# One denominator product per block for all groups and heads, and a turn at the tile's end, in a two-layer graph attention kernel

## The chip, the cores and the metric

The kernel runs on one core of a Trainium2 chip. The metric is the device time of one execution in microseconds (us), as a median of several runs. A profile is one execution, recorded by the hardware profiler, with the start and length of each instruction and of each DMA packet.

## The reference

The input has 3327 nodes with 1024 features and an adjacency matrix that is symmetric, has a full diagonal and is sparse: about 16 edges per node. There are two layers, each of the form x = layernorm(x + attention(x)).

```python
# layer 0: 8 heads of 128
h = (x @ W).reshape(C, H, D)
e = leaky_relu(alpha_src[:, :, None] + alpha_dst[:, None, :], 0.2)   # alpha = h . a, per head
attn = softmax(where(adj == 0, -inf, e), axis=-1)
out = einsum('hij,hjd->hid', attn, h_heads)
x = layernorm(x + out)
# layer 1: one head of 1024
h = x @ W1
att = softmax(where(adj > 0, leaky_relu(f1 + f2.T), -9e15), axis=1)  # f = h . a1, h . a2
x = layernorm(x + relu(att @ h))
```

For each target node and each head, layer 0 needs two sums over the node's edges: the weighted sum of the sources' rows, and the sum of the weights alone, which is the softmax's denominator. The change is about the second.

## The kernel before

The nodes are padded to 26 tiles of 128 targets. A first phase (`proj`) multiplies x with the weights, writes the rows of layer 0 to `h0_d` (1024 features and 16 exponentials of scores), and turns the adjacency matrix into lists of edges: for each tile `NB` = 17 lists of 128 edges, in `idx` (source row), `tgt` (target) and `re_d` (the target's factor per head). A tile's 128 targets form `NG` = 4 groups of `GT` = 32. Each of the `EB` = 4 blocks holds one list of 128 edges for each group; the 17th list, the end block, takes what is left over for the whole tile. If the lists would not suffice, another arm of the program (`by_pairs`) would run; here it does not.

The phase `sparse` has two stages, both under `pipeline`, with the order of the instructions on each engine written out by hand (`tc.manual_schedule`): the instructions stand on an engine's queue in the order in which Python issues them. The first stage has `Layer0` for its tiles and runs from about 482 to 1185 us of the span; the second has `Target` (layer 1).

For a tile t and block b, `pipeline` issues: at b = 0 `own()` of this tile; then `weights(b + 1)` (after the last block `weights(0)` of the next tile); then `sums(b)`; then the gathers of block b of the next tile; then one step of `work`, the `finish` of the tile before; and, while there are any, one step of `ahead` (`score_weights`, L767, at the start of layer 0).

- `gather` (L803): four indirect DMAs of 128 rows each, one per group, from GpSimd's queue into one of five buffers `src`; the end block has one such DMA into one of two buffers `end`.
- `weights` (L858): VectorE makes the edge's weight per head, `wp` (L865, L866), ScalarE copies it to `w` (L868), and VectorE spreads it over a one-hot matrix of the targets, `e` (L870): 128 edges x (4 groups x 8 heads x 32 targets).
- `sums` (L876): for each head and group a product `e`^T x rows into the group's 32 partitions of `acc` (L898); for the end block a product over all 128 partitions per head (L882). At b = 1 and 2 the tile's own rows, scaled by ScalarE in `own` (L850), are added by a product with the identity (L890), which stands ahead of that block's sums on TensorE.
- The denominators (L904 to L910): for each block and group, the one-hot matrix of the group's edges (`oh`, 128 x 32) is the stationary side, and the weights (`w`, 128 x 8) are the moving side; the result goes to the group's 32 partitions of `den`, which is 128 targets x 8 heads. Block 0's products are issued with block 1's; the end block has one product over all targets (L886). `den` has a single PSUM buffer (tag "S", one bank).
- `finish` (L915): the denominators' inverse `ri` (L918, L919); per head, the sums are scaled by it and added to x in `y` (L924); a step ends; statistics and square root (L192 to L195); a step ends; normalisation (L199) and a first score product (L931); a step ends; a second score product (L931), two exponentials (L936, L937), and the store of the row to `y_d`, on SP's queue (L938). Layer 1's gathers read `y_d`.

`pipeline` runs one step of `finish` after each block (`behind` is one for each), so that tile t's four steps follow the blocks 0 to 3 of tile t + 1; the last tile's steps run after the loop.

Of the kernel before, what the change touches and what calls it, by code (L numbers as in the profile page):

```python
# [9 lines left out]
F32 = mybir.dt.float32  # L10
# [3 lines left out]
AF = mybir.ActivationFunctionType  # L14
OP = mybir.AluOpType
AX = mybir.AxisListType
# [3 lines left out]
P = 128  # L20
# [6 lines left out]
def kernel(  # L27
# [28 lines left out]
    nc = tc.nc  # L56
    N, D = x.shape
    H, DH = a0_src.shape
# [10 lines left out]
    GT = 32  # L69
    NG = P // GT  # L70
    EB = 4
# [30 lines left out]
    ident = const.tile([P, P], F32, name="ident")  # L102
# [54 lines left out]
    class Phase:  # L157
# [7 lines left out]
        def bank(self, tag, shape, name, dt=F32):  # L165
            return self.psum.tile(shape, dt, tag=tag, name=name, bufs=self.banks[tag])

        def sbuf(self, tag, shape, bufs, name=None, dt=F32):
            return self.pool.tile(shape, dt, tag=tag, name=name or tag, bufs=bufs)
# [283 lines left out]
    with ExitStack() as own, tc.manual_schedule():  # L453
        ph = Phase(own, "proj", {"A": 2, "S": 1, "T": 2})
        pool, bank = ph.pool, ph.bank
# [205 lines left out]
        for t in range(3, NT):  # L661
# [3 lines left out]
            if t == 12:  # L665
                n, own = NT - 1, pool.tile([P, NT], I32, bufs=1, name="own")
# [76 lines left out]
    def sparse(own):  # L743
        ph = Phase(own, "sparse", {"A": 5, "S": 1, "T": 1, "E": 1})
        pool, bank, sbuf = ph.pool, ph.bank, ph.sbuf
# [14 lines left out]
        nc.vector.memset(none_b, 0.0)  # L760
        io_t = ph.iota([P, P], [[1, P]], "io_t", base=1)


        wc = pool.tile([P, 2, KT], F32, bufs=1, name="wc")
        wa = [pool.tile([P, D], F32, bufs=1, name=f"wa{n}") for n in range(2)]
# [60 lines left out]
        class Layer0:  # L826
# [31 lines left out]
            def weights(self, b):  # L858

                s = self.src[b]  # L860
                ng, wide = (NG, GT) if b < EB else (1, P)
                blk = slice(b * NG, b * NG + ng)
                oh = self.oh[:, blk, :] if b < EB else self.oh2.unsqueeze(1)
                wp = way[:, (b % 4) * NG * H : (b % 4 * NG + ng) * H].rearrange("p (g h) -> p g h", g=ng)
                nc.vector.tensor_tensor(wp, s[:, :, D : D + H], self.re[:, blk, :], OP.mult)  # L865
                nc.vector.tensor_tensor(wp, wp, s[:, :, D + H : D + 2 * H], OP.max)  # L866
                w = sbuf("w", [P, NG, H], 4)[:, :ng]
                nc.scalar.activation(w, wp, AF.Copy)  # L868
                e = sbuf("e", [P, H * P], 3).rearrange("p (g h t) -> p g h t", g=ng, h=H)
                nc.vector.tensor_tensor(  # L870
                    e, oh.unsqueeze(2).to_broadcast([P, ng, H, wide]),
                    wp.unsqueeze(3).to_broadcast([P, ng, H, wide]), OP.mult,
                )
                self.made[b] = w, e

            def sums(self, b):  # L876
                w, e = self.made[b]
                rowsof = self.src.pop(b)[:, :, :D].rearrange("p g (h d) -> p g h d", h=H)
                first = b == 0
                if b == EB:  # L880
                    for h in range(H):
                        nc.tensor.matmul(  # L882
                            self.acc[h // 4][:, h % 4, :], e[:, 0, h, :], rowsof[:, 0, h, :],
                            start=False, stop=h % 4 == 3,
                        )
                    nc.tensor.matmul(self.den, self.oh2, w[:, 0, :], start=False, stop=True)  # L886
                    return

                if b in (1, 2):
                    nc.tensor.matmul(  # L890
                        self.acc[b - 1].rearrange("p h d -> p (h d)"), ident, self.h[:, (b - 1) * HALF : b * HALF],
                        start=False, stop=False,
                    )
                elif b == 3:
                    nc.tensor.matmul(self.acc[0][:, 0, :1], ident_b, none_b, start=False, stop=False)
                for h in range(H):
                    for g in range(NG):
                        nc.tensor.matmul(  # L898
                            self.acc[h // 4][g * GT : (g + 1) * GT, h % 4, :], e[:, g, h, :], rowsof[:, g, h, :],
                            start=first and h % 4 == 0, stop=False,  # L900
                        )

                if b == 1:
                    self.den = bank("S", [P, H], "den")  # L904
                for n in (0, 1) if b == 1 else (b,)[: b]:
                    for g in range(NG):
                        nc.tensor.matmul(
                            self.den[g * GT : (g + 1) * GT, :], self.oh[:, n * NG + g, :], self.made[n][0][:, g, :],
                            start=n == 0, stop=False,
                        )  # L910

            def close(self):
                pass

            def finish(self):  # L915

                ri = sbuf("ri", [P, H], 2)
                nc.vector.tensor_tensor(ri, self.den, self.es, OP.add)  # L918
                nc.vector.reciprocal(ri, ri)  # L919
                t, row = self.t, self.y  # L920
                y = row[:, :D]
                for h in range(H):
                    yh = y[:, h * DH : (h + 1) * DH]
                    nc.vector.scalar_tensor_tensor(  # L924
                        yh, self.acc[h // 4][:, h % 4, :], ri[:, h : h + 1], yh, op0=OP.mult, op1=OP.add
                    )
                yield
                yield from ph.norm_steps([y])
                for n in range(2):
                    pr = sbuf("pr", [P, D], 1)  # L930
                    nc.vector.scalar_tensor_tensor(  # L931
                        pr, y, 1.0, wa[n], op0=OP.mult, op1=OP.mult, accum_out=r1.sd[:, t, n, :]
                    )
                    if n == 0:
                        yield
                nc.scalar.activation(row[:, D + 1 : D + 2], r1.d[:, t, :], AF.Exp)  # L936
                nc.scalar.activation(row[:, D + 2 : D + 3], r1.d[:, t, :], AF.Exp, scale=SLOPE)  # L937
                nc.sync.dma_start(y_d[t * P : (t + 1) * P, :], row)  # L938
# [267 lines left out]
    with arm.Else():  # L1206
        with ExitStack() as own:
            sparse(own)
# [23 lines left out]
```

## Time and profile before

| | us |
|---|---|
| median of 3 runs | 1957.28 |
| lowest, highest | 1956.42, 1968.05 |
| the profiled execution | 1903.19 |
| its span | 1901.5 |

In the profiled execution TensorE is busy for 1518.5 us (80%), VectorE for 1146.6, GpSimd for 1030.2 and ScalarE for 546.6. The granted clock of TensorE is 0.905 on average, about 0.8 in layer 0's edge stage and 1.0 in layer 1. The DMA engines read 578.85 MB and write 42.97 MB.

The engines are named PE (TensorE), DVE (VectorE), ACT (ScalarE), POOL (GpSimd) and SP; PEld is PE's weight load. A group's line names the source line, the engine, the operation, destination<-sources, the shapes, the number, then busy us and mean ns. A line of waits tells who waited for whom, with the total in us, the number of times and the longest. A line of the chain has a start, a length, and what ran or was waited for. A line of the timeline has a start, a length, engine, source line, operation, destination<-sources and the number; in brackets the idle time before it and what ended that.

### The profile page before, as it was taken

How to read it: one execution, taken by the hardware profiler on the slowest of the kernel's cores; microseconds unless marked ns; L12 is line 12 of the kernel's file. 1: busy time of each engine (PE TensorE's matmuls, PEld its weight loads, DVE VectorE, ACT ScalarE, POOL GpSimd, SP SyncE). 2: the span in 40 equal slices, each digit the busy share in tenths (PEclk: the TensorE clock that was granted, in tenths of full speed). 3: DMA queues.
4: the chain of work that ended last, by engine and by line, in shares of the span. 5: the costliest groups of instructions: out<-in, count | busy, mean ns of one | idle time of the engine just before them, and what ended most of it. 6: DMA issues, size and time to landing. Idle time of an engine off the chain costs nothing.

```text
span 1901.5 us, 38079 instructions
## 1 busy us (share of the span) xinstructions
PE 1518.5 (80%) x14663; PEld 902.4 (47%) x14663; DVE 1146.6 (60%) x3058; ACT 546.6 (29%) x1422; POOL 1030.2 (54%) x1391
## 2 busy tenths in 40 slices
PE   8799999999266555656556565399999999999997
PEld 5465556666255554545545454144444444444443
DVE  6699999986386665666666666244444444444442
ACT  5544455542022222222222222012222212222220
POOL 4322222220576666676676764677766667666650
PEclk9899999999678777787788877699999999999999
DMA  7656455411899999999999997899999999999980
GB/s 184 101 133 131 100 99 99 88 62 39 325 373 404 396 392 394 366 405 392 386 392 389 394 376 273 332 398 410 400 372 382 380 378 369 359 371 373 366 326 33
DMA packets 171068, 567.76 MB, mean 299 GB/s; under 512 B 27690, under 2 KB 34346, under 8 KB 170878
## 3 DMA queue, kind: packets, MB, share of 16 engines
q0 software_dynamic: 131056, 455.68, 67.6%
q1 hardware_dynamic: 39822, 109.56, 15.4%
q8 instruction: 118, 1.93, 0.4%
q14 instruction: 72, 0.59, 0.1%
HBM read 578.85 MB, written 42.97 MB: 327 GB/s over the span
## 4 chain that ended last, share of the span: by engine, by line
PE 52%; DMA 24%; DVE 12%; ACT 6%; issue 4%; POOL 2%; SPq 0%; DVEq 0%; ACTq 0%; POOLq 0%
DMA src<-h_d,idx 20%; PE mm L1025 20%; PE acc L993 12%; PE mm L479 12%; DVE e L870 3%; PE acc L898 3%; ACT junk L311 3%; PE tr L176 2%; POOL src L803 2%; DMA src<-y_d,idx 2%; DVE pr L931 1%; PE acc L882 1%; DMA wt<-in_L_gnn_W_dram 1%; ACT xT L179 1%; PE xp L411 1%
## 5 line engine op out<-in xcount | busy, mean ns | idle before, releaser
L803 POOL DMA_INDIRECT src<-h_d,idx x416 | 441.1, 1060 | 209.1 <-PE acc L898 58.0
L803 POOL DMA_INDIRECT src<-y_d,idx x416 | 415.7, 999 | 221.6 <-PE acc L993 96.3
L898 PE MATMUL acc<-src,e 128*32 128x128 f32 x6656 | 278.5, 337 | 253.6 <-DVE e L870 253.5
L479 PE MATMUL mm<-wt,xT 128*128 128x347 f32 (+1 forms) x1248 | 402.3, 469 | 3.3 <-DMA wt<-in_L_gnn_W_dram 2.9
L1025 PE MATMUL mm<-wt,xT 128*128 128x512 f32 x832 | 383.3, 604 | 0.8 <-DVE o L1028 0.8
L898 PEld LDWEIGHTS acc<-src,e 128*32 128x32 f32 x6656 | 234.8, 137 | 311.3 <-DVE e L870 284.3
L479 PEld LDWEIGHTS mm<-wt,xT 128*128 128x128 f32 x1248 | 228.3, 192 | 106.0 <-issue 4.2
L1025 PEld LDWEIGHTS mm<-wt,xT 128*128 128x128 f32 x832 | 152.2, 190 | 199.5 <-issue 179.1
L993 PE MATMUL acc<-src,es 128*32 128x342 f32 (+1 forms) x2496 | 206.2, 464 | 33.8 <-DVE es L984 31.0
L870 DVE TENSOR_TENSOR e<-oh,way 128x1024 f32<-128x1024 f32 x130 | 158.7, 1221 | 63.2 <-ACT w L868 62.8
L993 PEld LDWEIGHTS acc<-src,es 128*32 128x32 f32 x2496 | 71.6, 111 | 158.6 <-issue 112.9
L868 ACT ACTIVATE w<-way 128x32 f32<-128x32 f32 (+1 forms) x130 | 24.6, 189 | 407.7 <-DVE way L866 395.6
L1028 DVE SCALAR_TENSOR_TENSOR o<-mm,y 128x512 f32<-128x512 f32 x52 | 35.9, 691 | 166.2 <-PE mm L1025 166.2
L1007 ACT ACTIVATE z<-y,ri 128x342 f32<-128x342 f32 (+1 forms) x78 | 39.5, 570 | 313.9 <-DVE ri L1003 313.9
L865 DVE TENSOR_TENSOR way<-src,re 128x32 f32<-128x32 f32 x104 | 20.8, 200 | 175.1 <-DMA src<-h_d,idx 157.6
L179 ACT ACTIVATE xT<-tr 128x512 f32<-128x512 f32 x104 | 59.4, 596 | 151.0 <-PE tr L176 150.9
L981 DVE TENSOR_TENSOR way<-way,src 128x128 f32<-128x128 f32 x104 | 31.1, 299 | 90.0 <-ACT way L951 44.2
L850 ACT ACTIVATE own<-own,es 128x128 f32<-128x128 f32 x208 | 63.6, 388 | 57.4 <-DVE es L847 57.4
L311 ACT ACTIVATE junk<-ad 128x3328 uint8<-128x3328 uint8 x26 | 78.4, 3014 | 2.5 <-POOL ad L308 2.5
L882 PE MATMUL acc<-end,e 128*128 128x128 f32 x416 | 67.7, 328 | 13.3 <-DVE e L870 13.3
L296 POOL CAST mvs<-r 128x8 bf16<-128x8 f32 x26 | 6.0, 232 | 122.8 <-ACT r L295 122.8
L335 POOL TENSOR_TENSOR place_of<-cnt 128x1 f32<-128x1 f32 x26 | 4.9, 190 | 121.0 <-ACT cnt L328 101.5
(188 smaller groups left out, 1959.7 us busy)
## 6 DMA issues: line engine op xcount, KB each, us to landing
h_d<-ht SPq DMA_DIRECT2D x26, 520.0 KB
own<-h_d SPq DMA_DIRECT2D x26, 520.0 KB
y_d<-y SPq DMA_DIRECT2D x26, 514.0 KB
y<-y_d SPq DMA_DIRECT2D x26, 514.0 KB
x<-in_x_dram SPq DMA_DIRECT2D x25, 512.0 KB
y<-in_x_dram SPq DMA_DIRECT2D x25, 512.0 KB
out_dram<-o SPq DMA_DIRECT2D x25, 512.0 KB
ad<-in_adj_dram POOLq DMA_DIRECT2D x25, 415.9 KB
```

The lines of the kernel that those rows point to most:

```text
L176: nc.tensor.transpose(tr[:, k, :], src[:, (4 * g + k) * P : (4 * g + k + 1) * P], ident)
L179: nc.scalar.activation(part, tr, AF.Copy)
L311: nc.scalar.activation(junk, ad, AF.Copy, accum_out=self.deg)
L479: nc.tensor.matmul(acc, xT[t][:, k, :], wt[:, k, CUTS0[c] : CUTS0[c + 1]], start=k == 0, stop=k == KT - 1)
L803: nc.gpsimd.indirect_dma_start(out=s[:, g, :w], out_offset=None, in_=table[:, :], in_offset=bass.IndirectOffsetOnAxis(ap=idx[:, t, b * NG ...
L850: nc.scalar.activation(hn, hn, AF.Copy, scale=es[:, n : n + 1])
L870: nc.vector.tensor_tensor(e, oh.unsqueeze(2).to_broadcast([P, ng, H, wide]), wp.unsqueeze(3).to_broadcast([P, ng, H, wide]), OP.mult,)
L882: nc.tensor.matmul(self.acc[h // 4][:, h % 4, :], e[:, 0, h, :], rowsof[:, 0, h, :], start=False, stop=h % 4 == 3,)
L898: nc.tensor.matmul(self.acc[h // 4][g * GT : (g + 1) * GT, h % 4, :], e[:, g, h, :], rowsof[:, g, h, :], start=first and h % 4 == 0, stop= ...
L993: nc.tensor.matmul(self.acc[c][to, :m], es[:, g, :], s[:, g, CUTS[c] : CUTS[c + 1]], start=b == 0, stop=b == EB,)
L1007: nc.scalar.activation(z[:, cut], self.res[:, cut], AF.Copy, scale=ri[:, 1:2])
L1025: nc.tensor.matmul(acc, xT[:, k, :], wt1[:, k, half], start=k == 0, stop=k == KT - 1)
```

## The change

A block's denominators are now one product for all groups and heads: `w` (128 edges x 32 columns, group by head) is the stationary side, and the whole one-hot matrix (128 edges x 128 targets) is the moving side. The result has group and head in the partitions (32) and the targets in the columns; of each row only the 32 columns of its own group mean anything. The end block's weights are copied four times (`to_broadcast`), so that its product has the same form. In `finish`, VectorE multiplies the 32 x 128 result with a mask, `meets`, that keeps each group's own targets, into `met`; and a further product turns `met` by a 32 x 8 matrix `heads` of ones into 128 targets x 8 heads, in columns of the same bank. A `yield` after that makes `finish` five steps in place of four. Mask and `heads` are made once from the identity.

```diff
@@ sparse
+        meets = pool.tile([NG * H, P], F32, name="meets")
+        nc.vector.tensor_reduce(meets..., ident[: NG * H, : NG * H]..., AX.X, OP.max)
+        nc.vector.tensor_copy(meets...[:, :, 1:], meets...[:, :, :1].to_broadcast(...))
+        heads = pool.tile([NG * H, H], F32, name="heads")
+        nc.vector.tensor_reduce(heads, ident[: NG * H, : NG * H].rearrange("p (g h) -> p h g", g=NG), AX.X, OP.max)
@@ weights
-                w = sbuf("w", [P, NG, H], 4)[:, :ng]
-                nc.scalar.activation(w, wp, AF.Copy)
+                w = sbuf("w", [P, NG, H], 4)
+                nc.scalar.activation(w, wp if b < EB else wp.to_broadcast([P, NG, H]), AF.Copy)
@@ sums
-                    nc.tensor.matmul(self.den, self.oh2, w[:, 0, :], start=False, stop=True)
+                    nc.tensor.matmul(
+                        self.den[: NG * H, :P], w.rearrange("p g h -> p (g h)"), self.oh2, start=False, stop=True
+                    )
...
-                    self.den = bank("S", [P, H], "den")
+                    self.den = bank("S", [P, P + H], "den")
                 for n in (0, 1) if b == 1 else (b,)[: b]:
-                    for g in range(NG):
-                        nc.tensor.matmul(
-                            self.den[g * GT : (g + 1) * GT, :], self.oh[:, n * NG + g, :], self.made[n][0][:, g, :],
-                            start=n == 0, stop=False,
-                        )
+                    nc.tensor.matmul(
+                        self.den[: NG * H, :P], self.made[n][0].rearrange("p g h -> p (g h)"),
+                        self.oh[:, n * NG : (n + 1) * NG, :].rearrange("p g t -> p (g t)"),
+                        start=n == 0, stop=False,
+                    )
@@ finish
+                met = sbuf("met", [NG * H, P], 2)
+                nc.vector.tensor_tensor(met, self.den[: NG * H, :P], meets, OP.mult)
+                nc.tensor.matmul(self.den[:, P:], met, heads, start=True, stop=True)
+                yield
                 ri = sbuf("ri", [P, H], 2)
-                nc.vector.tensor_tensor(ri, self.den, self.es, OP.add)
+                nc.vector.tensor_tensor(ri, self.den[:, P:], self.es, OP.add)
```

More of the change, by code (lines that the diff above doesn't have):

```diff
@@ L761, in sparse @@
         io_t = ph.iota([P, P], [[1, P]], "io_t", base=1)
+        meets = pool.tile([NG * H, P], F32, name="meets")
+        nc.vector.tensor_reduce(
+            meets.rearrange("p (g t) -> p g t", g=NG)[:, :, 0], ident[: NG * H, : NG * H].rearrange("p (g h) -> p g h", g=NG),
+            AX.X, OP.max,
+        )
+        nc.vector.tensor_copy(
+            meets.rearrange("p (g t) -> p g t", g=NG)[:, :, 1:],
+            meets.rearrange("p (g t) -> p g t", g=NG)[:, :, :1].to_broadcast([NG * H, NG, GT - 1]),
+        )
+        heads = pool.tile([NG * H, H], F32, name="heads")
+        nc.vector.tensor_reduce(
+            heads, ident[: NG * H, : NG * H].rearrange("p (g h) -> p h g", g=NG), AX.X, OP.max
+        )
         wc = pool.tile([P, 2, KT], F32, bufs=1, name="wc")
@@ L885, in sums @@
                         )
-                    nc.tensor.matmul(self.den, self.oh2, w[:, 0, :], start=False, stop=True)
+                    nc.tensor.matmul(
+                        self.den[: NG * H, :P], w.rearrange("p g h -> p (g h)"), self.oh2, start=False, stop=True
+                    )
                     return
@@ L903, in sums @@
                 if b == 1:
-                    self.den = bank("S", [P, H], "den")
+                    self.den = bank("S", [P, P + H], "den")
                 for n in (0, 1) if b == 1 else (b,)[: b]:
-                    for g in range(NG):
-                        nc.tensor.matmul(
-                            self.den[g * GT : (g + 1) * GT, :], self.oh[:, n * NG + g, :], self.made[n][0][:, g, :],
-                            start=n == 0, stop=False,
-                        )
+                    nc.tensor.matmul(
+                        self.den[: NG * H, :P], self.made[n][0].rearrange("p g h -> p (g h)"),
+                        self.oh[:, n * NG : (n + 1) * NG, :].rearrange("p g t -> p (g t)"),
+                        start=n == 0, stop=False,
+                    )
             def close(self):
```

## The prediction

> **What bounds the kernel now.** The edit touches layer 0's edge stage alone, which runs from the first gather at 482 us to about 1185 us. I first read the busy table in stretches (columns: stretch, length, busy us of PE, its weight loads, DVE, ACT, POOL, then PE clock, DMA share, GB/s).
>
> ```profile
> 555.00:560.00 5.00, 5.00 (x147) 4.62 (x147) 4.59 (x9) 1.46 (x2) 1.67 (x2) 0.85 0.59 215
> 850.00:950.00 100.00, 59.51 (x1171) 50.17 (x1172) 63.04 (x154) 23.12 (x65) 67.15 (x65) 0.76 1.01 391
> 1170.00:1185.00 15.00, 11.04 (x246) 9.62 (x246) 12.44 (x30) 4.16 (x9) 0.00 (x0) 0.86 0.25 97
> ```
>
> In the body of the stage the 16 DMA engines are full (share 1.01, 391 GB/s) while no compute engine passes 67%. Two places differ: a dip at 555 us, and the last 15 us, where the gathers are over. Then the waits of PE, and the chain of waits in the body.
>
> ```profile
> PE acc L898 <- DVE e L870: 237.6, 93, 6.3
> ...
> 888.49 8.95 DMA src<-h_d,idx
> 897.44 0.02 issue
> 897.47 0.02 POOLq L803
> 897.48 0.01 issue
> 897.49 9.66 DMA src<-h_d,idx
> ```
>
> PE spends 237.6 us waiting for the edge weights `e`. In the chain a gather lands and releases the next one: transfer follows transfer, about 10 us each, with compute only now and then between. The question is then whether a later PE would hold a gather back. A gather of block b writes the buffer read five blocks before. The timeline shows how long that buffer has been free (L803 is a gather, L898 the block sums, L907 the denominators, L890 the injection of the own row, L918 the start of `finish`):
>
> ```profile
> 902.52 0.16 DVE L918 TENSOR_TENSOR ri<-den,es 128x8 f32<-128x8 f32 x1
> 902.66 1.95 PE L898 MATMUL acc<-src,e 128*32 128x128 f32 x64 [1.35 <-DVE e L870]
> 903.98 0.99 POOL L803 DMA_INDIRECT end<-h_d,idx  x1 [0.30 <-issue]
> 904.43 0.29 PE L907 MATMUL den<-w,oh 128*32 128x8 f32 x16
> 918.37 1.70 POOL L803 DMA_INDIRECT src<-h_d,idx  x1 [0.30 <-PE acc L898]
> 926.05 1.13 PE L890 MATMUL acc<-own,ident 128*128 128x512 f32 x2
> ```
>
> `sums(1)` ends at 904.61. After the `end` gather at 903.98 come eight gathers, the next tile's blocks 0 and 1, and then, at 918.37, the first that needs block 1's buffer: 13.8 us later. Counted alike from the same timeline, blocks 0, 2 and 3 give 12.4, 11.7 and 12.1 us. So in the body PE may be some 10 us late before DMA loses anything. The name PE behind 0.30 us of idle time is misleading: 0.30 stands before gathers that wait for nothing, too. At 558 us it is not so: there POOL stood 4.15 us behind PE, while the step-wise `score_weights` filled DVE.
>
> [...]the denominators' 8 columns have a median of 176 ns, the sums' 128 columns 273. [...]LDWEIGHTS (loading the stationary operand):[...] here 113 ns for 32 columns, 192 for 128.[...] the full 5 us stretches here show 403 to 412[...].
>
> **The change, part by part.** A product shows as two instructions (104 blocks x 4 groups = 416 products, 832 rows).
>
> *Removed:* per tile 16 group products and one of the end block, 34 rows. The 16 rows at 904.43 took 0.30 us with their loads at full clock (19 ns each), eight at half clock 0.41 us. That is 0.6 to 1.6 us for the groups, 0.4 for the end: 1.0 to 2.0 us a tile.
>
> *Added products:* five of 32 columns by 128 moving, 10 rows. The sums run 64 such rows in 1.95 us, 30 ns each with four column groups side by side; the new ones use one group, so up to 122 ns each, or 227 at half clock (64 in 3.64 us). That is 1.2 to 2.3 us a tile, and 0.3 if they overlap fully with the sums. Against what goes, PE's gain or loss is below 1 us a tile, under 237.6 us of waiting: zero. If PE bounded, it would be at most 26 us either way.
>
> *The mask and the turn:* one DVE product of 32x128 out of PSUM, between 166 ns (128x8, L846) and 299 ns (128x128 out of PSUM, L982); I take 0.30. The turning product is like L886 (loads 0.30 us, products 0.29, overlapping): 0.40 us.
>
> *A step more in `finish`:* its first part now holds only mask and turn; the head scaling (eight L924, 2.16 us), statistics, normalisation and the two score products each move one block later on DVE, as do square root, exponentials and the `y_d` store on ACT and SP. The sum is the same. Two stores keep their order on SP: `y_d` still goes before the next `re`, and the `x` and `own` loads follow later. POOL's queue is not touched.
>
> *New waits.* In the built order the turn stands on PE between `sums(0)` and the injection of block 1, and waits for the mask, which stands on DVE behind `e` of block 1. The injection, which ran before `e` was there (926.05, with the sums at 928.95), now queues behind: mask 0.30 + turn 0.40 + injection 1.12 (2.08 at half clock) = 1.9 to 2.9 us on `sums(1)`. Second, the next tile's first denominator waits for `ri`, which has moved behind `e` of block 2. So after that `e`: `ri` 0.2, two products 0.5, injection 1.1 = 1.8 us on `sums(2)`, 3.1 at half clock. Third, the second score product now precedes `own`: 1.3 us on DVE and two exponentials on ACT delay the eight own-row scalings (2.44 us), behind which block 1's copy of `w` stands; where DVE has no gap, up to 1.7 us more. Together `sums(1)` may be 2 to 4.6 us late, and `sums(2)` 2 to 3. Nobody waits behind them but PE itself and the gathers, which have 11.7 us or more: zero in the body. Without that cover it would be some 3 us x 25 tiles = 75 us.
>
> *At 555 us* there is no cover. The transposes of `score_weights` on PE now queue behind the denominator that waits for `ri`, and DVE does head scaling (2.5 us with its two small steps) in place of statistics (1.7). I take +1.5 us; bounds 0 and the 4.6 above.
>
> *At the end of the stage* all is on the path:
>
> ```profile
> 1181.77 1.23 DVE e L870
> 1183.00 0.04 issue
> 1183.05 2.05 PE acc L882 x16
> 1185.10 0.14 PE den L886 x2
> 1185.23 0.02 issue
> 1185.26 0.18 DVE ri L918
> ```
>
> Then comes the last tile's `finish`, its store, and layer 1's first gathers. `e` of block 3 was ready at 1178.96. New order: statistics 1.7, weights of the end block 1.9 (`e` at 1182.5, half a us sooner), end sums and denominator 2.3 (1184.8); DVE meanwhile normalises (2.1) and, only now, does the second score product (1.3): 1186.0. Mask 0.30, turn 0.40, gaps 0.1: `ri` at 1186.8 instead of 1185.26. +1.5 us; bounds +1 and +3 (a late `sums(2)`).
>
> *Setup:* three small DVE operations before the first `oh`; DVE then idles 7.69 us for `re`. Zero.
>
> **Sum.** 0 + 1.5 + 1.5 = +3. The profiled execution took 1903.19 us (span 1901.5); it would take 1906.2. The median of the three runs, 1957.28, is 54 us above the profiled one, which no view explains; I carry the 3 us over: 1960.3, rounded to 1960.
>
> **The rivals.** A change of 1% is 19.6 us, about what a measurement of this kernel tells from none.
>
> *A, forecast: covered by the full DMA, 1960 (0.80).* Own range 1954 to 1968.
>
> *B, slower: the buffers come free too late after all.* For it: where POOL really stood behind PE, as at 558 us, DMA fell to 215 GB/s; half-clock tiles make each delay longer. Against it: 11.7 us of reserve. It decides once the delays add up from block to block to more than the reserve; then a third of the 75 us would show: 1957 + 25 + 3 = 1985 (0.13).
>
> *C, faster: the dips get smaller.* Between 550 and 1150 us the mean is 389 GB/s against 407 in full stretches, 4.4% of 600 us = 26 us. If fewer PE rows and DVE work spread otherwise fill half of it: 1957 + 3 - 13 = 1947 (0.07). For it: the end block's `e` comes sooner. Against it: most dips have a share of 1.0, so the engines are full with smaller pieces.
>
> That the change does less than it says is excluded: the built program has 130 denominator products and 26 turns, where there were 442 products.
>
> **Numbers.** To leave out no more than two in ten, the range goes from 1953 (part of C, and what runs differ by) to 1973 (part of B, and early and final bounds of 4.6 and 3). Faster by over 1%: the far part of C, 0.03. Slower: most of B, 0.10. Within: 0.87.
>
> **What the changed profile would show.** DMA share near 1.0 and about 390 GB/s in the body; 12 us reserves shrunk to 8 or 10, gathers still following landings; a PE wait of `den` on `ri` and of the turn on the mask, with block sums 2 us or more behind their `e`; the last `ri` about 1.5 us after its end sums would have allowed. Wrong if: the body's GB/s falls below 380 with POOL idle over 1 us behind PE, or the stage ends over 10 us earlier.

## The result, and the profile after

| | us |
|---|---|
| before, median of 22 runs beside the changed kernel | 1959.06 (1952.59 to 1970.13) |
| changed, median of 22 runs | 1946.93 (1943.52 to 1957.23) |
| ratio | 0.9946, 95% interval 0.9931 to 0.9962 |
| the changed kernel's profiled execution, its span | 1954.92, 1953.2 |

The change makes the kernel 12 us faster. Forecast were 1960 us and no gain. The number of the third rival, 1947, was hit, but by luck and not for its reason: the transfers' mean rate between 550 and 1150 us is 372 GB/s, so no filled dip made the kernel faster. The profiled execution is one of the longer ones, 8 us above the median.

The stretch that stood for the body of the stage, in the changed kernel (columns as before: PE, its weight loads, DVE, ACT, POOL, PE clock, DMA share, GB/s):

```profile
850.00:950.00 100.00, 79.03 (x1125) 51.82 (x1125) 63.22 (x155) 25.71 (x75) 67.45 (x62) 0.85 1.00 373
```

The DMA engines are still busy all the time, but they move 373 GB/s where they moved 391, and PE is busy 79% where it was 60%. The shares of the chain that ended last, by engine over the whole span, in the profile before and in this one, and then this one's waits of PE between 550 and 1150 us:

```profile
PE 52%; DMA 24%; DVE 12%; ACT 6%; issue 4%; POOL 2%; SPq 0%; DVEq 0%; ACTq 0%; POOLq 0%
...
PE 74%; issue 10%; DVE 6%; ACT 5%; DMA 2%; another core or an unknown queue 1%; POOL 1%; SPq 0%; POOLq 0%; DVEq 0%; ACTq 0%
```

```profile
PE acc L914 <- issue: 124.4, 294, 1.1
PE acc L914 <- PE acc L914: 0.8, 3, 0.3
```

DMA had 24% of the chain before and has 2% now. PE no longer waits for `e` at all. Instead it stands still 294 times ahead of a block's product, 124.4 us in all, with "issue" as the cause: for nothing that the profile shows. The timeline of one block's sums shows what that looks like (L914 is the block sums, L935 the turn, L938 the start of the scaling):

```profile
922.72 0.46 PE L914 MATMUL acc<-src,e 128*32 128x128 f32 x6 [0.38 <-issue]
...
924.88 0.46 PE L914 MATMUL acc<-src,e 128*32 128x128 f32 x4 [0.98 <-issue]
...
926.31 0.38 PE L914 MATMUL acc<-src,e 128*32 128x128 f32 x3 [0.97 <-issue]
...
929.80 0.59 PE L935 MATMUL den<-heads,met 32*128 32x8 f32 x2
...
930.43 0.17 DVE L938 TENSOR_TENSOR ri<-den,es 128x8 f32<-128x8 f32 x1 [5.36 <-PE den L935]
```

The block's sums began at 920.55, so its operands were there. A few products run, PE stands for 0.4 or 1.0 us, a few more run. The 64 product rows took 1.95 us in one piece in the profile before; here they go on until 929.87. And it is DVE now that waits for PE, 5.36 us for the turn.

This is not what the change did. The kernel before shows it too in runs on other chips, as the experiments will tell.

### The profile page after: what moved, and what is told of

It is laid out like the page before. It is cut to its first block, busy times and chain, and to the rows that moved or that the text cites. A ratio compares the mean times of both kernels' runs of the same rounds, so it can differ in the third digit from the quotient of the medians.

```text
span 1953.2 us, 36865 instructions
## 1 busy us (share of the span) xinstructions
PE 1668.2 (85%) x14091; PEld 915.1 (47%) x14091; DVE 1151.9 (59%) x3087; ACT 546.6 (28%) x1422; POOL 1039.7 (53%) x1391
## 3 DMA queue, kind: packets, MB, share of 16 engines
q8 instruction: 113, 1.85, 0.4%
## 4 chain that ended last, share of the span: by engine, by line
PE 74%; issue 10%; DVE 6%; ACT 5%; DMA 2%; another core or an unknown queue 1%; POOL 1%; SPq 0%; POOLq 0%; DVEq 0%; ACTq 0%
PE mm L1045 19%; PE acc L914 19%; PE acc L1013 13%; PE mm L479 12%; PE acc L906 4%; PE acc L896 3%; ACT junk L311 3%; PE tr L176 2%; DMA wt<-in_L_gnn_W_dram 1%; DMA src<-h_d,idx 1%; PE den L922 1%; PE xp L411 1%; DVE top L274 1%; PE den L935 1%
## 5 line engine op out<-in xcount | busy, mean ns | idle before, releaser
L817 POOL DMA_INDIRECT src<-h_d,idx x416 | 448.9, 1079 | 228.0 <-PE acc L914 83.1
L914 PE MATMUL acc<-src,e 128*32 128x128 f32 x6656 | 396.2, 321 | 167.0 <-issue 138.1
L914 PEld LDWEIGHTS acc<-src,e 128*32 128x32 f32 x6656 | 254.1, 127 | 332.5 <-issue 309.4
L1013 PE MATMUL acc<-src,es 128*32 128x342 f32 (+1 forms) x2496 | 215.9, 467 | 39.2 <-DVE es L1004 24.9
L882 ACT ACTIVATE w<-way 128x32 f32<-128x32 f32 x130 | 25.0, 193 | 449.1 <-PE acc L914 177.2
L906 PE MATMUL acc<-own,ident 128*128 128x512 f32 x104 | 81.0, 871 | 0.0
L1021 DVE TENSOR_TENSOR ri<-acc,es 128x1 f32<-128x1 f32 x26 | 4.1, 158 | 124.3 <-PE acc L1013 116.7
L938 DVE TENSOR_TENSOR ri<-den,es 128x8 f32<-128x8 f32 x26 | 4.3, 166 | 119.8 <-PE den L935 119.8
```

The source lines that it names most:

```text
L817: nc.gpsimd.indirect_dma_start(out=s[:, g, :w], out_offset=None, in_=table[:, :], in_offset=bass.IndirectOffsetOnAxis(ap=idx[:, t, b * NG ...
L906: nc.tensor.matmul(self.acc[b - 1].rearrange("p h d -> p (h d)"), ident, self.h[:, (b - 1) * HALF : b * HALF], start=False, stop=False,)
L914: nc.tensor.matmul(self.acc[h // 4][g * GT : (g + 1) * GT, h % 4, :], e[:, g, h, :], rowsof[:, g, h, :], start=first and h % 4 == 0, stop= ...
L1013: nc.tensor.matmul(self.acc[c][to, :m], es[:, g, :], s[:, g, CUTS[c] : CUTS[c + 1]], start=b == 0, stop=b == EB,)
```

## The experiments

The runs fall into six groups, each on a chip of its own with the kernel before beside it. The kernel before had medians of 1902.01, 1978.50, 1957.32, 1979.69, 1901.96 and 1960.74 us there. Two kinds stand apart: at 1902 us, and at 1957 to 1980 us. I call them the quicker and the slower kind. No chip was used for two groups, so whether the kind belongs to the chip, or to something else that held while a group ran, isn't known.

A ratio is to the kernel before of the same group. It isn't the quotient of the two medians, and differs from it by up to 0.0022; so differences of 5 us between kernels with few runs mean little.

"Rows" are PE's rows in the trace, products and weight loads together. A product of f32 shows as two products and two loads, four rows: the 3328 products of the block sums are 6656 product rows and 6656 loads in the profile before, and as many in the changed one. (The prediction counts the product rows alone: its 34 are 68 here.) The edge stage has 622 rows a tile before and 578 after, since the denominators have 24 in place of 68.

### The quicker kind

**The kernel before, unchanged.**

> The kernel before, unchanged, for a profile of an ordinary execution: the one at hand took 1903 us, the runs 1953 to 1970. If instruction supply to TensorE is what holds the edge stage of layer 0 (theory I), its trace shows gaps of about 0.7 us between the products of one block's sums, with nothing awaited, and an edge stage some 12 us longer than that of the changed kernel. If the stage is bound by the gathers as in the profile at hand (theory II: the order of the finish steps made the difference), TensorE waits for e, as there. Ratio to itself 1.000.

Measured: 1901.89, ratio 0.9999 (0.9987 to 1.0011). The span's stages are those of the profile before.

**The order alone:** an empty first step in the `finish` of the kernel before.

```diff
             def finish(self):
+                yield
                 ri = sbuf("ri", [P, H], 2)
```

> The kernel before with one empty first step in finish: all finish steps a block later, and the next tile's first denominators wait for ri, as in the changed kernel; products and their number as before. Theory I (fewer instructions on TensorE): no gain, 1957 to 1962 us. Theory II (the order): 1945 to 1949 us, the whole gain.

Measured: 1901.20, 0.9993 (0.9982 to 1.0003).

**The products alone:** the changed kernel without its new `yield`.

```diff
                 nc.tensor.matmul(self.den[:, P:], met, heads, start=True, stop=True)
-                yield
                 ri = sbuf("ri", [P, H], 2)
```

> The changed kernel without the new step: mask, turn, and the scaling follow each other in one step, so the finish steps stand where they stood before; VectorE waits there for the turn. Theory I: the gain stays, 1944 to 1949 us. Theory II: it is gone, 1957 to 1962 us.

Measured: 1898.81, 0.9984 (0.9975 to 0.9993).

**Fewer products:** the kernel before without the denominator products of blocks 1 to 3, 48 rows less a tile, which leaves those blocks out of the denominators.

```diff
-                for n in (0, 1) if b == 1 else (b,)[: b]:
+                for n in (0,) if b == 1 else ():
```

> The kernel before without the denominator products of blocks 1, 2 and 3 (left out: those parts of the denominators); 48 of some 622 TensorE instructions per tile less, nothing else moved. The changed kernel has 44 less. Theory I: 1943 to 1948 us. Theory II: 1955 to 1960 us.

Measured: 1898.94, 0.9981 (0.9970 to 0.9993). The last three expectations name times for a kernel before of about 1957 us, so this kind decides nothing between their theories. Here the order is worth nothing that can be told, and fewer rows are worth 3 us.

**The changed kernel itself** met this kind in a later group.

> The changed kernel again, as the measure for the run before on the same chip: 0.990 to 0.996 of the kernel before where that takes 1955 us or more, 0.997 to 0.999 where it takes about 1902 us.

Measured: 1897.67 against 1901.96, 0.9980 (0.9971 to 0.9989). PE's longest wait in the profile before, and then its waits of this run, between 550 and 1150 us:

```profile
PE acc L898 <- DVE e L870: 218.4, 86, 6.3
...
PE den L935 <- DVE met L934: 96.3, 23, 4.4
PE acc L914 <- DVE e L884: 85.4, 43, 4.9
PE acc L896 <- DVE e L884: 17.0, 14, 1.4
PE den L922 <- DVE ri L938: 3.6, 6, 1.0
```

This is the picture that the prediction drew: the turn waits for the mask, the next denominator for `ri`, and what PE waits there it no longer waits for `e`. What follows on PE queues behind the new wait: in this run the turn starts at 874.57 us, after 4.28 us of waiting for the mask, the injection at 875.10 and `sums(1)` at 877.10. No wait ahead of a block's product is put down to "issue". The time is 4.3 us less, where +3 was forecast.

### The slower kind: the kernel before shows the pauses too

> The kernel before, for a profile from a chip where it takes over 1950 us, if these runs get one. There: gaps of some 0.7 us between products of one block with nothing awaited, as in the changed kernel's trace, the last gather of layer 0 some 12 to 16 us later than in the changed kernel, layer 1 as long as there. On a chip where it takes about 1902 us: the known profile once more. Ratio 1.000.

Measured: 1956.30, 0.9986 (0.9966 to 1.0006), unchanged as it should be. The pauses came as expected. The last gather of layer 0 did not: it starts at 1194.6 us, and in the changed kernel's profile, from another chip, at 1193.2, where 12 to 16 us between them were expected. PE's waits between 550 and 1150 us, and two windows of the same run:

```profile
PE acc L898 <- issue: 126.1, 316, 1.1
PE den L907 <- issue: 3.1, 8, 0.5
```

```profile
850.00:950.00 100.00, 74.88 (x1118) 49.33 (x1111) 58.97 (x145) 24.34 (x74) 63.59 (x62) 0.88 0.99 373
...
1196.00:1212.00 16.00, 15.24 (x320) 13.08 (x319) 11.08 (x28) 3.11 (x10) 0.00 (x0) 0.79 0.35 139
```

The pauses are in the kernel before as in the changed one. In the stage's last tile, when the gathers are over and the DMA share is 0.35, PE is busy for 15.24 of 16 us and gets through 20 product rows in a us. (In the body it is 11.2, but that tells little alone: the quicker kind has 11.7 there, with PE waiting for `e`.) The first phase, with a mean DMA share of 0.49 in the profile before, takes as long on both kinds: the first gather comes at 482.3 us in the profile before and at 483.4 here. So PE is held up by something other than its operands. That it is the supply of instructions is a guess, to which I come back.

The pauses of layer 0 are not all of the difference between the kinds. The gathers of layer 0 take 711 us from the first to the last where they took 687 in the profile before; those of layer 1, which the change doesn't touch, take 667 where they took 641. About half of the 53 us thus lies in layer 1. What makes that longer stays open.

### How much of the gain is the number of rows

**The changed kernel with 24 empty products a tile** (32 x 1 in bf16, so a product and a load each, as the 26 bf16 products of the profile before show with 26 rows and 26 loads: 48 rows), and, on the same chip, **with the denominators' block products over 384 columns in place of 128** (as many rows, longer):

```diff
+                if b:
+                    for n in range(8):
+                        nc.tensor.matmul(self.acc[0][:GT, 0, :1], ident_b[:, :GT], none_b, start=False, stop=False)
```

```diff
-                        self.den[: NG * H, :P], self.made[n][0].rearrange("p g h -> p (g h)"),
-                        self.oh[:, n * NG : (n + 1) * NG, :].rearrange("p g t -> p (g t)"),
+                        self.den[: NG * H, : 3 * P].rearrange("p (c t) -> p c t", c=3),
+                        self.made[n][0].rearrange("p g h -> p (g h)"),
+                        self.oh[:, n * NG : (n + 1) * NG, :].rearrange("p g t -> p (g t)").unsqueeze(1).to_broadcast([P, 3, P]),
...
```

> The changed kernel, unchanged, on whatever chip these runs get: chips differ (before takes 1959 us on the one of the result, 1902 on the one of the first four experiments). Theory I' (it pays where TensorE itself is late, which depends on the chip): ratio 0.994 where before takes about 1959, and 0.997 to 1.001 where it takes about 1902. Theory II' (a gain that does not depend on the chip): 0.994 on both.

> The changed kernel with 24 empty products per tile (32 columns by 1 moving column, adding zeros) and their weight loads: 48 TensorE instructions, as many as the change saves, with little working time. If the number of instructions counts: the gain is lost, as slow as before. If only working time counts: within 5 us of the changed kernel, 26 at most.

> The changed kernel with each block's denominator product over 384 moving columns instead of 128 (the same columns three times, two thirds unused): 8 product rows per tile longer[...], and not one instruction more. If TensorE's working time counts: 20 to 50 us more than the changed kernel. If it is the number of its instructions: within 5 us of the changed kernel. If it is covered by the gathers: within 3 us.

Measured beside 1978.50: the changed kernel 1967.10, 0.9920 (0.9896 to 0.9944); with more rows 1984.61, 1.0032 (1.0018 to 1.0046); with longer products 1970.85, 0.9946 (0.9926 to 0.9966). The 1248 more rows cost 17.5 us by the medians, 14 ns each; by the ratios with their intervals it is 13 to 22. In the traces all of it lies in layer 0's edge stage: from its first gather to the first of layer 1 it takes 770.0 us with more rows and 753.3 without.

Three times the columns cost 3.8 us by the medians, with intervals that overlap. That is little for what was added: eight product rows a tile with a median of 486 ns in place of 273, 1.7 us a tile or 44 us in all if nothing ran beside them. (The 20 to 50 us of the expectation were the author's estimate.) The stretch of 550 to 1150 us and PE's waits in it show where it went, first in the changed kernel, then with the longer products:

```profile
550.00:1150.00 600.00, 460.05 (x6222) 293.00 (x6223) 362.41 (x891) 141.95 (x414) 397.42 (x365) 0.83 0.99 366
PE acc L914 <- issue: 132.3, 307, 1.2
...
550.00:1150.00 600.00, 477.85 (x6264) 283.37 (x6263) 361.13 (x890) 143.44 (x419) 397.18 (x365) 0.85 0.99 366
PE acc L914 <- issue: 118.9, 257, 1.2
```

PE is busy for only 17.8 us more, so part of the added time runs beside other rows; and it pauses for 13.4 us less, so most of the rest comes out of the pauses. With more rows the pauses don't shrink: 134.0 us.

**The kernel before without 48 rows a tile** (the edit of the fewer products above, and the same part of the denominators left out), beside the changed kernel:

> The kernel before without the denominator products of blocks 1 to 3, 48 TensorE instructions less a tile; those denominators are left out of the sum. No wider product, no turn, no new order. Theory (14 ns for each instruction, 1248 of them): about 17 us less, 0.991, where the kernel before takes 1955 us or more. Rival (the change gains by its order, and the number of products is nothing): 1.000. On a chip of about 1902 us both expect 0.998, as measured once.

> The changed kernel itself, beside the kernel before on one chip. Theory (the gain is the time in which TensorE stands still between products while the gathers fill the DMA engines, and shrinks with the number of its instructions): on a chip where the kernel before takes 1955 us or more, 0.990 to 0.996; on a chip where it takes about 1902 us, 0.997 to 0.999, since there TensorE waits for the gathered weights anyway. Rival (fewer products are worth their own duration, whatever the chip): 0.994 on either.

Measured beside 1979.69: fewer rows 1963.26, 0.9913 (0.9892 to 0.9934); the changed kernel 1967.53, 0.9944 (0.9922 to 0.9966). Here the same count, taken away, gives 16.4 us, 13 ns a row (10 to 17 by the interval), with nothing else changed. So fewer rows are enough for a gain of this size on the slower kind, and more rows take it away. At 13 to 14 ns the change's 44 rows a tile (1144 in all) are worth 15 to 16 us; by the medians it gained 9 to 12.

Why a row costs this isn't shown. It isn't the pace of the pauses, which is some 150 ns a row in the slow stretches shown further down. It lies within what such short rows take in the profile before, as the prediction read it: 16 product rows with their loads in 0.30 us at full clock (1.00 granted), 9 ns a row, and eight in 0.41 us at half clock (0.50), 26 ns a row. So the two runs with more and with fewer short rows don't tell their number from their own time on PE; only the longer products speak for the number.

### Where the rest of it went

**The order alone, and the products alone**, beside the kernel before of 1957.32:

> The empty first step of finish alone, products as before. If the number of TensorE instructions is the whole of the gain: ratio 0.998 to 1.003 on any chip. If the order has a part in it on a chip of the slower kind: 0.993 to 0.997 there.

> The changed products with the finish steps where they were before (mask, turn and scaling in one step). If the number of TensorE instructions is the whole of the gain: 0.990 to 0.995 on a chip of the slower kind (0.998 on the other, as measured there). If the order has a part in it: 0.996 to 0.999.

Measured: order 1965.71, 1.0049 (1.0028 to 1.0070); products 1954.03, 0.9979 (0.9962 to 0.9996). The order alone costs 8 us, more than either expectation had; the products alone fall where the order was to have a part. The changed kernel was not run in this group. It had 0.9920, 0.9944 and 0.9958 in the three others of this kind and 0.9946 in the result, and the intervals of some of these overlap with that of the products alone. So it isn't clear that the products alone gain less. That something is given back shows best above: with its 44 rows put back and four more, the changed kernel is at 1.0032 (1.0018 to 1.0046), not at 1.

With the order alone PE pauses longer, 140.7 us in 600 where the kernel before on the same chip had 126.1:

```profile
PE acc L898 <- issue: 140.7, 329, 1.1
```

With the turn in the same step as the scaling, DVE stands for the next tile's first sums. DVE's waits, products alone:

```profile
DVE ri L937 <- PE den L935: 61.9, 20, 7.1
...
DVE met L934 <- PE acc L914: 49.5, 18, 3.2
```

The changed kernel has 113.6 us of waits of `ri` for the turn in the same stretch, on another chip, so the `yield` has not taken DVE's standing away either. Two attempts followed.

**The turned denominators in a buffer of their own**, so that the next tile's first denominator product needn't wait for `ri`:

```diff
-                    self.den = bank("S", [P, P + H], "den")
+                    self.den = bank("S", [P, P], "den")
...
-                nc.tensor.matmul(self.den[:, P:], met, heads, start=True, stop=True)
+                dent = bank("T", [P, H], "dent")
+                nc.tensor.matmul(dent, met, heads, start=True, stop=True)
...
-                nc.vector.tensor_tensor(ri, self.den[:, P:], self.es, OP.add)
+                nc.vector.tensor_tensor(ri, dent, self.es, OP.add)
```

> The changed kernel with the turned denominators in a PSUM buffer of another tag, so that the next tile's first denominator product no longer waits until VectorE has read this tile's turned ones. Theory (that wait lies on TensorE's path where TensorE paces the stage): 0.1 to 0.4% below the changed kernel of the same chip, 2 to 8 us. Rival (the wait is over before TensorE gets there): within 0.1% of the changed kernel.

Measured: 1970.01, 0.9954 (0.9941 to 0.9967), the changed kernel on that chip 0.9944. No gain, as the rival had it: in the changed kernel's trace from this chip PE has no wait for `ri` between 550 and 1150 us.

**The turn halfway through the next tile's first sums**, the mask ahead of them, the scaling back in its old step:

```diff
                 for h in range(H):
+                    if first and h == H // 2 and turns:
+                        turns.pop()()
...
+            def meet(self):
...
+                turns.append(lambda: nc.tensor.matmul(self.den[:, P:], met, heads, start=True, stop=True))
...
-                yield
...
+                    if b == 0 and t and kind is Layer0:
+                        tiles[t - 1].meet()
                     tg.sums(b)
```

> The changed kernel with the mask computed ahead of the next tile's first sums and the turning product issued halfway through them (after four of the eight heads), and the scaling back in the step where the kernel before has it. TensorE's instructions are as many as in the changed kernel. Theory (of the gain of the fewer instructions, about 17 us where TensorE's pauses pace the stage, the changed kernel loses some by VectorE's waiting for the turn behind the first sums): the wait of ri for the turned denominators falls from 110 us in 600 us to below 60, and the time is 2 to 8 us below the changed kernel of the same chip. Rival (VectorE's waiting is only the slack that it has while TensorE paces the stage): the same time as the changed kernel within 2 us, the wait moved to e. On a chip of about 1902 us both expect 0.997 to 0.999 of the kernel before.

> The same kernel as e15_turn_inside, with the turn halfway through the next tile's first sums. On a chip where the kernel before takes 1955 us or more: theory (VectorE's waiting for the turn behind the first sums gives part of the gain away) 2 to 8 us below the changed kernel; rival (that waiting is slack) within 2 us of it. On a chip of about 1902 us: 1.000 of the kernel before, as e15 had.

> The changed kernel as the measure for the run before: 0.990 to 0.996 of the kernel before where that takes 1955 us or more; 0.998 where it takes about 1902 us, as e16 had.

Measured on the quicker kind: 1902.21, 1.0001 (0.9990 to 1.0012), where 0.997 to 0.999 was expected and the changed kernel had 0.9980. On the slower kind, beside 1960.74: 1963.65, 1.0020 (1.0003 to 1.0037), where the changed kernel had 1951.87, 0.9958 (0.9940 to 0.9976). DVE's longest waits with the turn inside:

```profile
DVE e L886 <- PE den L926: 43.6, 16, 5.7
DVE met L937 <- PE acc L918: 39.3, 15, 5.6
DVE ri L946 <- PE acc L918: 37.3, 14, 4.3
```

The wait for the turn is almost gone (8.7 us), as expected, and the gain with it. The theory fell: DVE's standing behind the turn was not what ate the rest. DVE stands as before, under other names. Why this order costs 12 us against the changed kernel, with its pauses ahead of the sums hardly changed (125.3 us, 126.9 in the changed kernel on the same chip), and why the `yield` alone costs 8 with longer ones, these traces don't tell. It stays open.

### Are full DMA engines the condition?

**Three gathers in place of four:** the kernel before, with block 3 of layer 0 computed from the rows gathered for block 2. Block 3's own rows are left out.

```diff
-                self.src[b] = gather(h0_d, HW0, self.t, b)
+                self.src[b] = self.three if b == 3 else gather(h0_d, HW0, self.t, b)
+                self.three = self.src[b]
```

> The kernel before with block 3 of layer 0 computed from the rows gathered for block 2; block 3's gather is left out, a quarter of the gathered blocks of layer 0. TensorE's instructions are the same. Theory (TensorE's pauses between products come only while the gathers fill the DMA engines): the pauses with nothing awaited fall from 120 to 140 us in 600 us to below 30 us where the kernel before shows them, and layer 0 shortens by 50 us or more, to TensorE's own 22 to 24 us a tile. Rival (they belong to TensorE and its clock, not to the DMA engines): the pauses stay above 100 us in 600 us, and layer 0 shortens by less than 20 us there.

Measured: 1947.36 beside 1979.69, 0.9845 (0.9818 to 0.9872), 32 us less, between the two expectations; and the pauses stayed: 110.4 us ahead of the sums, and 37.1 ahead of the denominators. By the expected numbers the theory lost: the rival had the pauses right, and neither had the time. Inside this run, though, the pauses can be set against the DMA share, which is no longer 1.0 throughout. Windows of the run (columns as above), two stretches with pauses and two without:

```profile
907.27:916.02 8.75, 3.10 (x29) 1.46 (x29) 1.83 (x5) 1.01 (x5) 6.04 (x6) 0.80 0.99 331
916.02:926.67 10.65, 10.37 (x207) 8.69 (x206) 7.48 (x21) 4.01 (x11) 2.17 (x3) 0.84 0.73 268
...
934.64:943.37 8.73, 3.44 (x28) 1.41 (x28) 1.71 (x5) 0.89 (x5) 5.92 (x6) 0.80 1.01 344
943.37:954.12 10.75, 10.43 (x209) 8.84 (x209) 7.62 (x21) 4.01 (x11) 2.20 (x3) 0.85 0.67 234
```

and its timeline at the border:

```profile
914.59 0.29 PE L908 MATMUL den<-w,oh 128*32 128x8 f32 x4 [0.57 <-issue]
916.02 0.16 PE L896 MATMUL acc<-none_b,ident_b 128*128 128x1 bf16 x1 [1.14 <-issue]
916.11 3.50 PE L899 MATMUL acc<-src,e 128*32 128x128 f32 x64
```

With a DMA share of 1.0 PE gets 28 or 29 product rows in 8.7 us; with 0.7 it gets 207 or 209 in 10.7 us, six times as many in a us. The three gathers left still fill the engines for part of each tile, and that part is where PE crawls. So full DMA engines are a condition of the pauses, or go with it: POOL has six gathers in each of the slow stretches and three in each of the others, and this run can't separate the two. They are not a sufficient one: the quicker kind has a share of 1.01 and no pauses.

The slow stretches show one thing more. The engines are as full as in the profile before, but they move 331 and 344 GB/s, not 391. Transfers and PE are slow together there. Whether one slows the other, or a third thing both, no run here has tested.

That PE's instructions come late when the gathers fill the engines would fit the pauses, and is the author's guess. The profiles list transfers of kind "instruction": the larger of their two queues has 118 packets and 1.93 MB before, 113 and 1.85 MB after, so 16.4 KB each. Which engine's instructions these are, no view tells. The guess is not shown: the pauses come in trains, 0.7 us or twice that apart, 294 of them between 550 and 1150 us of the changed kernel on the slower kind, where there are 50 such packets; a packet takes about 1 us there (0.5% of the 16 engines' 600 us), as on the quicker kind (56 packets, 0.6%, in the profile before); and no run here has slowed or moved these transfers.

## Why the prediction was wrong

*The body, "under 237.6 us of waiting: zero".* Right to 4 us on the quicker kind, which the profile's 1903 us belong to: 0.9980, with the new waits where they were foretold. Wrong for the runs that counted. There PE waited for `e` not at all, so the cover of 237.6 us was not there.

*"The median of the three runs, 1957.28, is 54 us above the profiled one, which no view explains; I carry the 3 us over."* This is the step that failed. The 54 us were not a constant that can be added: in executions of that length PE doesn't wait for `e` but pauses ahead of the sums, "issue", 126.1 us in 600, in the kernel before as after. Only a profile of such an execution shows it. With that known, the sentence "If PE bounded, it would be at most 26 us either way" was the one to price: 44 rows a tile at 13 to 14 ns are 15 to 16 us, less what was given back, and the change gained 12.

*The price of the products.* I set 1.0 to 2.0 us a tile that go against 1.2 to 2.3 us that come, and got about zero. On the slower kind the first term was about right: 12 of the 16 group products left out gave 16.4 us, 0.63 us a tile. The second was too large: making the block products 1.7 us a tile longer cost 3.8 us in all, 0.15 us a tile, and perhaps nothing. Its 122 ns a row were the author's estimate, four times the 30 ns of rows of four groups side by side; it fits the profile before, where 64 rows of 32 columns take 1.95 us and 16 rows of 128 columns 2.05, 128 ns each. Few long products for many short ones are thus a gain there and not a draw.

*The medians of 8 and 128 columns.* 176 and 273 ns show only that a product's time isn't proportional to its columns. A later run adds a third: the empty products of one column, in bf16, have a median of 163 ns.

*The gathers' reserve* (rival B). On the quicker kind it held. On the slower one it was used up before the change: in the kernel before POOL stands behind PE's sums and denominators for 77.2 and 60.0 us in 600, where it was 53.6 and 8.9 in the profile before. (Of each wait 0.3 us stand before any gather.) The rival's 25 us did not come all the same.

*The late steps at 555 us and at the stage's end, +1.5 each.* Not to be told on the quicker kind. Between 555 and 560 us the changed kernel moves 186 GB/s, where two runs of the one before move 215 and 280. From the last gather of layer 0 to the first of layer 1 it takes 31.9 us, where they take 29.7 and 32.1.

*Rival C, the dips.* GB/s between 550 and 1150 us is 393 on the quicker kind, 389 before: 1%, which fits the 4 us there. It doesn't explain the 12 us: on the slower kind the mean is 372, and 373 in the kernel before.

*What the changed profile would show.* The `den` on `ri` and the turn on the mask were seen on the quicker kind alone. The sign of being wrong, "the body's GB/s falls below 380 with POOL idle over 1 us behind PE", came true, and the kernel was faster all the same, as the kernel before is at 373 on such a chip.

## What to carry to other kernels

If a profiled execution is 3% shorter than the timed runs, as here, its waits may not be those of the timed runs: get a profile whose time fits before anything is hidden under its waits, or price the change under both bounds. Where PE stands between products with nothing awaited, a longer product may come out of the pauses and cost next to nothing, as the 384 columns did here (3.8 us for 44 added); then few wide products for many narrow ones can be a gain even if they take as long (12 us here). And an order that costs nothing where transfers pace a stage need not be free elsewhere: the `yield` cost nothing on one chip and 8 us on another.

## What was not expected of the hardware

Six chips ran the same kernel in 1902, 1902, 1957, 1961, 1978 and 1980 us. A lower clock is not the reason: granted were 0.907 and 0.908 on the mean of the runs of the quicker kind, and 0.914 to 0.916 of the slower. What makes the two kinds isn't shown. On the slower one, with the DMA engines full, PE's rows come in trains with pauses of up to 1.2 us: 294 of them and 124.4 us in 600 us of the changed kernel, 316 and 126.1 us of the kernel before. A short row more or less costs 13 to 14 ns there, and 213 ns more on each of eight product rows a tile cost 3.8 us in all, or nothing within the noise.
